# Two graph layers on one core: the squares moved into the aggregate's last pieces, the second layer's statistics put off by one more piece, one graph's channel sums and the second layer's weights read at other points

## The chip, the core and the metric

The kernel runs on one core of a Trainium2 chip. The core has a matrix engine (PE, with the weight loads shown apart as PEld), a vector engine (DVE), a scalar engine (ACT), a general engine (POOL) and a queue engine (SP) that only starts transfers; POOL starts transfers too. Every engine works through its own list of instructions in order and waits on semaphores for the others. The time is that of the whole program on the device, in microseconds; lower is better. Everything is float32.

## What is computed

Sixteen graphs of 1024 nodes with 256 channels share one 1024x1024 adjacency matrix. The first layer weighs the adjacency by a function of the channel means, forms queries from it, and does attention with four heads. The second layer multiplies by the normalised adjacency, applies a linear map, a normalisation over all graphs and nodes, a relu, a second linear map and a second normalisation.

```python
h = maximum(layernorm(x), 0)
c = mean(h, channels);  A = symmetric(2*||sigmoid(c_m - c_n) - .5| - .5|)
g = relu((h.T @ (adj * A)) * para)                 # queries, per graph
k, v = split(h @ kv_w);  x = x + softmax(g.T k) v  # 4 heads
h = maximum(layernorm(x), 0)
A_hat = dinv * (adj + I) * dinv                    # dinv from row and column sums
y1 = relu(batchnorm((A_hat @ h) @ W1.T + b1))
x = x + batchnorm(y1 @ W2.T + b2)
```

## The kernel before

One Python function records the instructions of all engines in the order in which they are to stand; nothing reorders them afterwards, so the order in the code is the order on each engine. The main body is `attention()`: for each graph b it goes through 16 steps of two score tiles and two value products, and between these it draws pieces from a generator, `background(b)`, which does everything else: keys, values and queries of graph b+1, and the second layer's aggregate (`aggregate`, seven products of a Strassen-like scheme, 14 pieces) and first linear map (`hidden`, two times seven products, 14 pieces) of graph b-1. In this text "stage b" is the stretch in which graph b has its attention. A stage in the middle takes some 135 us.

`weave(main, (start, side), ...)` takes one piece of each side generator with every piece of the main one, from piece number `start` on. `soon(action)` puts an action off until the next piece has been recorded: with one `soon`, an action stands on its engine behind the next piece's instructions. `weave`, `soon` and the counts in the calls are all that sets the order.

What the change touches:

- `squares(b)` (L432): two DVE transposes of 32x32 blocks (128x1024 each, L438), one for each half of the channels, into a tile `sq`, which a POOL transfer (L442) writes to DRAM; `gathered(b, k)` (L444) reads it back from there with four SP transfers (L450) as the transposed activations `ht` that the keys and values of the next stage take. `squares` is called in `prepare(b)` (L931) after two of `hidden`'s pieces, and it takes its tile from the pool tag "h" of two buffers, which also holds the activations of both layers.
- `summed(b)` (L926) is woven into the last eleven of the aggregate's pieces: the layernorm of graph b (eight pieces), then `differences(b)` (L454), which sends the channel sums through DRAM (L467) and reads them back as a row on all partitions, `cbc` (L471).
- `put` in `hidden` (L822) sends a finished 128x512 block of the second layer to DRAM and records its statistics (L825, DVE) one piece later. The products of `hidden` go to three PSUM buffers in turn (`bank`, L167): a product can start when the block of the product three before it has been taken out, which is done by DVE adds (L837, L842, L847, L860, L866) and ACT copies.
- `background(0)` (L949) weaves the queries of graph 1 with the pieces of `graph()` (POOL, the combined adjacency) and `degrees()` (column sums: loads of `at`, ACT at L241, DVE at L243 and L244), and calls `differences(2)` after all of them.
- `load_later()` (L303) reads the second layer's first weights (L305), forms four sums of them on POOL (L309 to L312), writes the 1024 values `dinv` to DRAM one by one (L314) and reads them back as a row on all partitions, `dbc` (L315), which has to wait for the write. It is called in stage 1, before the queries of graph 2. All its transfers stand on SP, in the same list as the loads of the adjacency (`adj`, L192), of `para` (L549) and of the aggregate's matrix (`aht`, L714).

Of the kernel before, what the change touches and what calls it, by code (L numbers as in the profile page):

```python
# [10 lines left out]
F32 = mybir.dt.float32  # L11
# [6 lines left out]
P = 128  # L18
# [5 lines left out]
def gnn_two_layers_kernel(  # L24
# [12 lines left out]
    nc = tc.nc  # L37
    B, N, C = x.shape
    H1 = w1_t.shape[1]
    NT = N // P  # L40
    CC = C // P
# [23 lines left out]
    stats1 = const.tile([P, HC, B * NH, 6], F32, name="stats1")  # L65
# [8 lines left out]
    hsq_d = [dram.tile([P, CC, N], F32, name=f"hsq_d{b}") for b in range(B)]  # L74
# [9 lines left out]
    SQ = 32  # L84
    NS = P // SQ
# [13 lines left out]
    def layers(shifted):  # L99
# [31 lines left out]
        def soon(action):  # L131

            queue.append(action)
# [17 lines left out]
        def weave(main, *sides):  # L151

            for i, cost in enumerate(main):
                for start, side in sides:
                    if i >= start:
                        cost += next(side, 0.0)
                yield cost
            for _, side in sides:
                yield from side

        def double(slots):

            for _ in slots:
                next(slots, None)
                yield 0.0
# [266 lines left out]
        def squares(b):  # L432

            sq = p2.tile([P, CC, N], F32, tag="h", name=f"sq_{b}")
            for k in range(CC):
                nc.vector.transpose(  # L438
                    sq[:, k].rearrange("p (i t s) -> p i t s", i=NS, s=SQ),
                    hs["a", b][:, :, k * P : (k + 1) * P].rearrange("p t (i s) -> p i t s", s=SQ),  # L440
                )
            nc.gpsimd.dma_start(out=hsq_d[b], in_=sq)  # L442

        def gathered(b, k):  # L444

            ht = p3.tile([P, N], F32, tag="ht", name=f"ht_{b}_{k}")
            hts.setdefault(b, []).append(ht)
            src = hsq_d[b][:, k].rearrange("(j s) (i r) -> i s j r", s=SQ, i=NS)
            for i in range(NS):
                nc.sync.dma_start(  # L450
                    out=ht[i * SQ : (i + 1) * SQ].rearrange("s (j r) -> s j r", j=NS), in_=src[i]
                )
# [342 lines left out]
        def hidden(b):  # L795

            if b >= B - 2:
                yield from plain_hidden(b)
                return
            HH = H1 // 2  # L800
            a11, a12, _, a22 = w1_quarters()
            s1, s2, s3, s4 = (later["s"][:, i] for i in range(4))
            b11, t3, b21, b22 = at_quarters(b)
            t1, t2 = steps[b]
            t4 = p2.tile([P, FB], F32, tag="para", name=f"at4_{b}")
            nc.gpsimd.tensor_sub(t4, b21, t2)

            def left(block, c):
                return block[:, c * P : (c + 1) * P]

            def one(name, block, c, right):
                part = bank(f"py_{b}_{c}_{name}")
                product(part, left(block, c), right, True, True)
                return part

            made = {}

            def new(name, c):
                made[name] = py.tile([P, FB], F32, tag="y", name=f"y_{b}_{c}_{name}")
                return made[name]  # L820

            def put(y, n, j):  # L822
                i = b * NH + n
                nc.gpsimd.dma_start(out=y1_d[i][:, j, :], in_=y)
                soon(lambda: nc.vector.bn_stats(stats1[:, j, i, :], y))  # L825

            add = nc.vector.tensor_add

            def m1(c):
                part = one("1", a11, c, b11)  # L830
                nc.scalar.activation(
                    new("11", c), part, AF.Identity, bias=b1[:, c : c + 1]
                )

            def m2(c):
                y = made["11"]
                add(y, one("2", a12, c, b21), y)  # L837
                put(y, 0, c)

            def m3(c):  # L840
                y = made["12"]
                add(y, one("3", s4, c, b22), y)  # L842
                put(y, 1, c)

            def m4(c):
                y = made["21"]
                add(y, one("4", a22, c, t4), made["sum"])  # L847
                put(y, 0, 2 + c)

            def m5(c):  # L850
                nc.scalar.copy(new("22", c), one("5", s1, c, t1))
                if c == 1:
                    both(c)

            def both(c):
                nc.gpsimd.tensor_add(new("12", c), made["21"], made["22"])

            def m6(c):
                y = new("21", c)
                add(y, one("6", s2, c, t2), made["11"])  # L860
                if c == 0:
                    both(c)

            def m7(c):
                part, y = one("7", s3, c, t3), made["22"]
                nc.vector.scalar_tensor_tensor(  # L866
                    new("sum", c), part, b1_step[:, c : c + 1], made["21"], op0=ALU.add, op1=ALU.add
                )
                nc.gpsimd.tensor_add(y, y, made["sum"])
                put(y, 1, 2 + c)  # L870

            for c, order in ((0, (m1, m5, m6, m2, m3, m7, m4)), (1, (m1, m6, m2, m5, m7, m3, m4))):
                for each in order:
                    each(c)
                    yield 0.86
# [50 lines left out]
        def summed(b):  # L926
            yield from Norm(b, True).all()
            differences(b)
            yield 0.0

        def prepare(b, products):  # L931


            w = weighers[b]
            yield from islice(products, 1)
            yield from islice(products, 1)
            squares(b)
            yield from weave(islice(products, 5), (0, islice(w, 2)))
            gathered(b, 0)
            yield from weave(islice(products, 3), (0, islice(w, 1)))  # L940
            gathered(b, 1)
            yield from weave(islice(products, 3), (0, islice(w, AHEAD - 3)))
            yield from products
# [3 lines left out]
        def background(b):  # L947

            if b == 0:  # L949
                differences(1)  # L950
                for k in range(CC):
                    yield TOP
                    transposed(1, (k,))
                    yield 1.0
                w, products, norm = weighers[1], keys_values(1), Norm(2, True).all()
                yield from weave(islice(products, 4), (0, double(islice(w, 8))))
                yield from weave(
                    plain_queries(1), (0, w), (4, norm), (5, graph()), (7, degrees())
                )
                differences(2)  # L960
                w = weighers[2]
                yield from islice(products, 1)
                yield from weave(islice(products, 2), (0, islice(w, 2)))
                yield TOP
                transposed(2, (0,))
                yield 1.0
                yield from weave(islice(products, 1), (0, islice(w, 1)))
                yield from islice(w, 1)
                yield TOP
                transposed(2, (1,))  # L970
                yield 1.0
                yield from islice(w, AHEAD - 4)
                yield from products
                return
            before = hidden(b - 1)
            gather = aggregate(b - 1)
            if b + 1 < B:
                w, products, norm = weighers[b + 1], keys_values(b + 1), normed(b - 1)
                yield from weave(islice(products, 4), (0, islice(w, 4)))
                if b == 1:  # L980
                    load_later()
                yield from weave(queries(b + 1), (0, double(w)), (9, islice(norm, 5)))
                yield next(gather)
                if b + 2 < B:
                    load_x(b + 2, True)
                yield from weave(products, (0, norm))
            else:
                yield next(gather)
                yield from weave(endings.pop(), (2, normed(b - 1)))
            if b + 2 < B:  # L990
                yield from weave(gather, (3, summed(b + 2)))
                yield from prepare(b + 2, before)
            elif b + 2 == B:

                yield from gather
                endings.append(before)
            else:
                yield from gather
                yield from weave(before, (0, normed_last()))
# [287 lines left out]
        with st:  # L1287
# [22 lines left out]
            else:  # L1310
# [7 lines left out]
                norm = Norm(0, True)  # L1318
# [369 lines left out]
```

## Time and profile before

| | |
|---|---|
| median of 3 runs | 2484.15 us (2481.71 to 2485.78) |
| the profiled execution | 2482.2 us, its span 2480.3 us |
| PE busy | 2418.3 us, 97% of the span |
| DVE busy | 1999.8 us, 81% |
| ACT busy | 1261.2 us, 51% |
| POOL busy | 565.2 us, 23% |

The page says that PE is busy in nearly the whole of the span. In the 40 slices PE stands at 9 tenths or more throughout, but for the last slice. So what an edit can give is found in the short stretches in which PE waits. The list of waits names them by the line that waited and the line that ended the wait; the timeline shows single instructions with start, duration, engine, line and, in brackets, the idle time before.

### The profile page before, as it was taken

To read this page: it belongs to the slowest core of one execution; us is meant where nothing else is said; L and a number is where in the kernel's file an instruction comes from. 1 tells how busy PE (TensorE), PEld (TensorE's weight loads), DVE (VectorE), ACT (ScalarE), POOL (GpSimd) and SP (SyncE) were. 2 spreads that over 40 slices of the span, in tenths; PEclk is the share of its full clock that TensorE was granted. 3 is DMA by queue.
4 is the path that set the end of the run, shared out by engine and by line. 5 is a ranking of instruction groups with operands and counts; after the bars stand their busy time and mean duration, and the time that the engine had idled before them with its cause. 6 is when DMAs were issued, how large, how long until landed. Compare 5 with 4: busy or idle time off the path is not lost. (4 is left out here: it accounts for less than half of the span.)

```text
span 2480.3 us, 35952 instructions
## 1 busy us (share of the span) xinstructions
PE 2418.3 (97%) x13290; PEld 829.3 (33%) x13290; DVE 1999.8 (81%) x3103; ACT 1261.2 (51%) x1870; POOL 565.2 (23%) x632
## 2 busy tenths in 40 slices
PE   9999999999999999999999999999999999999995
PEld 4333232332323232323323232323233232334444
DVE  5678887979798888889797978888897978767775
ACT  7764454545463645545454645355454534345554
POOL 1480202112121202021111212120201102136652
PEclk9999999999999999999999999999999999999997
DMA  4665535354555544453545555544535453456559
GB/s 145 198 218 175 181 124 191 120 198 157 181 174 191 168 168 162 144 181 118 210 143 175 170 191 170 187 160 148 177 126 197 133 199 122 157 205 222 192 198 373
DMA packets 202682, 437.19 MB, mean 176 GB/s; under 512 B 21248, under 2 KB 96512, under 8 KB 196736
## 3 DMA queue, kind: packets, MB, share of 16 engines
q1 hardware_dynamic: 173328, 327.29, 39.9%
q0 software_dynamic: 29168, 107.50, 11.4%
q8 instruction: 107, 1.75, 0.3%
q14 instruction: 79, 0.65, 0.1%
HBM read 331.36 MB, written 103.35 MB: 175 GB/s over the span
## 5 line engine op out<-in xcount | busy, mean ns | idle before, releaser
L1064 ACT ACTIVATE p<-sc 128x1024 f32<-128x1024 f32 x512 | 495.6, 1020 | 581.4 <-PE sc L1056 579.7
L1088 DVE TENSOR_TENSOR acc<-acc,p 128x1024 f32<-128x1024 f32 x384 | 469.5, 1223 | 81.6 <-ACT p L1064 60.3
L1056 PE MATMUL sc<-q,k 64*64 64x512 f32 x4096 | 500.1, 603 | 4.2 <-ACT p L1064 4.2
L1099 PE MATMUL o<-p,v 128*64 128x512 f32 x2048 | 494.6, 604 | 0.0
L174 PE MATMUL pa<-aht,h_b 128*64 128x512 f32 x1536 | 346.0, 592 | 1.1 <-ACT h_b L368 1.1
L174 PE MATMUL pg<-w,x_h 128*64 128x512 f32 x1472 | 332.0, 592 | 1.9 <-DVE x_h L579 1.9
L1056 PEld LDWEIGHTS sc<-q,k 64*64 64x64 f32 x4096 | 131.7, 132 | 340.9 <-issue 287.8
L1117 POOL DMA_DIRECT2D out_d<-os x58 | 33.9, 584 | 914.9 <-DVE os L1113 883.9
L1099 PEld LDWEIGHTS o<-p,v 128*64 128x64 f32 x2048 | 124.4, 136 | 297.9 <-issue 272.4
L493 DVE SCALAR_TENSOR_TENSOR w<-w,adj 128x1024 f32<-128x1024 f32 x128 | 166.2, 1306 | 31.9 <-ACT w L514 26.1
L174 PEld LDWEIGHTS pa<-aht,h_b 128*64 128x64 f32 x1536 | 110.0, 137 | 220.7 <-issue 208.8
L174 PEld LDWEIGHTS pg<-w,x_h 128*64 128x64 f32 x1472 | 105.6, 137 | 212.4 <-issue 201.0
L506 ACT ACTIVATE w<-cbc,csum 128x512 f32<-128x512 f32 x256 | 170.3, 716 | 4.7 <-DMA cbc<-csum_d 4.7
L514 ACT ACTIVATE w<-w 128x1024 f32<-128x1024 f32 x128 | 135.5, 1059 | 2.5
L569 DVE TENSOR_TENSOR w<-w,w 128x1024 f32<-128x1024 f32 x112 | 133.2, 1219 | 1.5
L174 PE MATMUL py<-at,w1s 128*64 128x512 f32 x448 | 109.5, 598 | 9.7 <-DVE y L837 7.5
L174 PE MATMUL pv<-kvw_f,ht 128*64 128x256 f32 x1024 | 116.1, 379 | 0.0
L174 PE MATMUL pk<-ht,kvw_f 128*64 128x512 f32 x512 | 115.2, 592 | 0.2 <-ACT ht L430 0.2
L174 PE MATMUL py<-at,w 128*64 128x512 f32 x464 | 113.3, 595 | 1.3 <-DVE at L727 0.7
L368 ACT ACTIVATE x_h<-x_h,lnsm_a 128x256 f32<-128x256 f32 x120 | 70.5, 593 | 74.6 <-DMA aht<-aht_d 67.1
L1085 DVE TENSOR_TENSOR acc<-p,p 128x1024 f32<-128x1024 f32 x64 | 79.2, 1237 | 31.5 <-ACT p L1064 31.5
L1428 ACT ACTIVATE yin_f<-yin_f,sm_f 128x512 f32<-128x512 f32 x128 | 93.5, 802 | 15.0 <-DMA yin_f<-y_d 14.9
(197 smaller groups left out, 2967.1 us busy)
## 6 DMA issues: line engine op xcount, KB each, us to landing
aht<-aht_d SPq DMA_DIRECT2D x224, 512.0 KB
adj<-in_adj_dram SPq DMA_DIRECT2D x128, 512.0 KB
y_d<-y POOLq DMA_DIRECT2D x128, 256.0 KB, 3.8
yin_f<-y_d SPq DMA_DIRECT2D x32, 1024.0 KB
para<-in_para_dram SPq DMA_DIRECT2D x64, 256.0 KB
x_d<-x_x POOLq DMA_DIRECT2D x16, 1024.0 KB, 5.1
xo_f<-x_d SPq DMA_DIRECT2D x32, 512.0 KB
out_dram<-xo_f POOLq DMA_DIRECT2D x32, 512.0 KB, 11.1
```

The lines of the kernel that those rows point to most:

```text
L174: nc.tensor.matmul(dst[r], left[:, r], right, start=start, stop=stop)
L368: nc.scalar.activation(self.h[:, t, :], self.src[:, t, :], AF.Relu, bias=self.sm[:, 1, t : t + 1], scale=self.sm[:, 0, t : t + 1], accum_o ...
L493: nc.vector.scalar_tensor_tensor(w, w, 1.0, a, op0=ALU.add, op1=ALU.mult)
L506: nc.scalar.activation(w[:, t, :].rearrange("p (t q) -> p t q", q=P), cbc[:, q * NT // NH : (q + 1) * NT // NH], AF.Abs, bias=csum[:, th * ...
L514: nc.scalar.activation(made[i], made[i], AF.Tanh, scale=-0.5 / C)
L569: nc.vector.tensor_sub(block(i)[part], block(x)[part], block(y)[part])
L1056: nc.tensor.matmul(sc[part, e, :], ks[b][k][r, m * P + c * HW : m * P + (c + 1) * HW], qs[b][k][r, f * FB : (f + 1) * FB], start=True, sto ...
L1064: nc.scalar.activation(pr, sc, AF.Exp)
L1085: nc.vector.tensor_add(self.acc, self.held, pr)
L1088: nc.vector.tensor_add(self.acc, self.acc, pr)
L1099: nc.tensor.matmul(self.o[r, :], vs[b][k][:, m, r], pr[:, e, :], start=(m == 0), stop=(m == NT - 1),)
L1428: nc.scalar.activation(y, y, AF.Relu, bias=sh[:, j : j + 1], scale=scale[:, j : j + 1])
```

## The change

Five edits:

1. `squares` becomes a generator of two pieces. Each half has a tile of its own tag "sq" with one buffer, its own transfer to DRAM, and a piece of its own.
2. It is called at the end of `summed`, beside the last two pieces of the aggregate, and no longer in `prepare`. There, `gathered(b, 0)` moves from after seven of `hidden`'s pieces to after two; `gathered(b, 1)` follows after eleven pieces where it followed after ten.
3. The statistics in `put` are put off by two pieces.
4. In `background(0)` the weave is cut after 13 of the 16 pieces of the queries, with 8 pieces of `graph` and 6 of `degrees`; then comes `differences(2)`, then the rest.
5. `load_later()` is called after the queries of graph 2, just ahead of the first loads of the aggregate.

```diff
-            sq = p2.tile([P, CC, N], F32, tag="h", name=f"sq_{b}")
             for k in range(CC):
+                sq = p1.tile([P, N], F32, tag="sq", name=f"sq_{b}_{k}")
                 nc.vector.transpose(
-                    sq[:, k].rearrange("p (i t s) -> p i t s", i=NS, s=SQ),
+                    sq.rearrange("p (i t s) -> p i t s", i=NS, s=SQ),
                     hs["a", b][:, :, k * P : (k + 1) * P].rearrange("p t (i s) -> p i t s", s=SQ),
                 )
-            nc.gpsimd.dma_start(out=hsq_d[b], in_=sq)
+                nc.gpsimd.dma_start(out=hsq_d[b][:, k], in_=sq)
+                yield 0.0
...
-                soon(lambda: nc.vector.bn_stats(stats1[:, j, i, :], y))
+                soon(lambda: soon(lambda: nc.vector.bn_stats(stats1[:, j, i, :], y)))
...
             yield from Norm(b, True).all()
             differences(b)
             yield 0.0
+            yield from squares(b)
...
             yield from islice(products, 1)
             yield from islice(products, 1)
-            squares(b)
-            yield from weave(islice(products, 5), (0, islice(w, 2)))
             gathered(b, 0)
+            yield from weave(islice(products, 6), (0, islice(w, 2)))
...
+                asked, build, sums = plain_queries(1), graph(), degrees()
                 yield from weave(
-                    plain_queries(1), (0, w), (4, norm), (5, graph()), (7, degrees())
+                    islice(asked, 13),
+                    (0, w),
+                    (4, norm),
+                    (5, islice(build, 8)),
+                    (7, islice(sums, 6)),
                 )
                 differences(2)
+                yield from weave(asked, (0, build), (0, sums))
...
+                yield from weave(queries(b + 1), (0, double(w)), (9, islice(norm, 5)))
                 if b == 1:
                     load_later()
-                yield from weave(queries(b + 1), (0, double(w)), (9, islice(norm, 5)))
                 yield next(gather)
```

## The prediction

> **What bounds the kernel.** The page comes first, then the list of waits for PE alone.
>
> ```profile
> PE 2418.3 (97%) x13290; PEld 829.3 (33%) x13290; DVE 1999.8 (81%) x3103; ACT 1261.2 (51%) x1870; POOL 565.2 (23%) x632
> ```
>
> ```profile
> PE py L174 <- DVE y L837: 7.5, 13, 0.6
> ...
> PE sc L1056 <- ACT p L1064: 4.2, 2, 3.7
> PE py L174 <- DVE y_sum L866: 2.2, 13, 0.2
> PE pg L174 <- DVE x_h L579: 1.9, 1, 1.9
> ```
>
> PE is the bound, and only its waits can be won. Two of the four rows come 13 times, once in each of stages 1 to 13, always equally long; the other two come once, in stages 0 and 1. These are the four places that the edits aim at. I then went through the timeline around each.
>
> Stage 1's `hidden`, on DVE, POOL and PE:
>
> ```profile
> 282.96 0.69 DVE L744 TENSOR_TENSOR at<-pa,at 128x512 f32<-128x512 f32 x1 [0.50 <-PE pa L174]
> ...
> 284.30 2.36 DVE L438 STREAM_TRANSPOSE sq<-x_h 128x1024 f32<-128x1024 f32 x2
> ...
> 287.54 1.29 POOL L856 TENSOR_TENSOR y<-y,y 128x512 f32<-128x512 f32 x1
> ...
> 289.28 2.55 DVE L1088 TENSOR_TENSOR acc<-acc,p 128x1024 f32<-128x1024 f32 x2
> ...
> 293.73 1.08 PE L174 MATMUL py<-at,w1s 128*64 128x512 f32 x4 [0.17 <-DVE y_sum L866]
> ...
> 301.82 1.08 PE L174 MATMUL py<-at,w1s 128*64 128x512 f32 x4 [0.57 <-DVE y L837]
> ```
>
> From L744 to L837 DVE has no gap above 0.3 us: PE waits for a full DVE queue. A product takes 0.86 us start to start (291.64 to 293.36 would be two), so the first stall is worth 0.37 and the second (due at 301.08, two products after 299.36) 0.74.
>
> Stages 0 and 1:
>
> ```profile
> 137.02 0.20 DVE L465 STREAM_TRANSPOSE csumt<-csum 128x32 f32<-128x32 f32 x1
> ...
> 148.26 1.33 ACT L506 ACTIVATE w<-cbc,csum 128x512 f32<-128x512 f32 x2 [4.70 <-DMA cbc<-csum_d]
> ...
> 152.05 3.40 PE L1056 MATMUL sc<-q,k 64*64 64x512 f32 x16 [3.71 <-ACT p L1064]
> ```
>
> ```profile
> 177.64 0.37 SPq L314 DMA_DIRECT2D dinv_d<-deg  x1
> ...
> 188.03 0.34 SPq L315 DMA_DIRECT2D dbc_f<-dinv_d  x1
> ...
> 196.46 1.23 DVE L493 SCALAR_TENSOR_TENSOR w<-w,adj 128x1024 f32<-128x1024 f32 x1 [4.75 <-DMA adj<-in_adj_dram]
> ```
>
> The row `cbc` comes late, ACT stands, and PE with it for 3.71 us; the scores after it take 3.40 where they take 1.95 elsewhere, because the granted clock is at half there. In stage 1 SP stands 10.4 us between L314 and L315 with two `adj` loads behind it; DVE waits 4.75 us for one, PE 1.95.
>
> **What the Trainium skill says.** "DMA: Bandwidth & Descriptors", "Rules for kernel authors": a transfer whose last dimension isn't contiguous has one descriptor per element, and one that reads what another wrote must wait for its semaphore. The trace agrees: 1024 values of 4 bytes took the 10.3 us above, and L315 waited. "SBUF — State Buffer", "SBUF: two separate sides": a DVE operation with two SBUF inputs and a GpSimd operation lock a shared port pair against each other, the later one blocks. Stage 2 shows it, where L856 happened to run over L1088:
>
> ```profile
> 424.31 1.29 POOL L856 TENSOR_TENSOR y<-y,y 128x512 f32<-128x512 f32 x1
> 424.75 3.27 DVE L1088 TENSOR_TENSOR acc<-acc,p 128x1024 f32<-128x1024 f32 x2
> ```
>
> The pair took 3.27 instead of 2.55, and PE lost 0.7 more in that stage. "TensorE: Matmul & The Clock Gate", "What's actually happening": an idle PE falls to half clock, about 3.4 us of work brings it back. The trace agrees once: 3.71 us idle cost 3.40 - 1.95 = 1.45 us more.
>
> **The change, part by part.** The orders of PE and ACT stay as they are; DVE, POOL and SP change.
>
> *Channel sums of graph 2.* L465 moves ahead of three pieces, behind L244 of the fifth `at` (ends 125.93). So `csum_d` starts at 126.1 instead of 137.25, and `cbc`, which followed it by 4.2 us and landed 6.8 us later, lands at about 137. ACT wants it at 143.6. The stall of 3.71 and its 1.45 us of half clock go: 5.2. On SP the last `at` load now stands behind these transfers; it starts near 130.7 instead of 125.9, and lands, 6 to 8 us later, at 137 to 139. ACT wants it at 132.42, so ACT stops there for some 5 us. Behind it stand L664, the two `v` copies and the next two exponentials, which end at 142 instead of 139.9; PE asks for their buffers at 144.5. The cover is 2.6 us; landing at 139 it costs up to 1.4 further on. I take 0.2. **Sum: -5.0.**
>
> *Second layer's weights.* The wait in stage 1's queries goes: -1.95. But L305, L314 and L315 now stand on SP just ahead of the five first `aht` loads. In stage 1 these start at 229.11 and PE takes the first at 239.87. In the later stages the whole SP sequence stands 2.1 us earlier against PE (last `para` 15.2 ahead of the first aggregate product, in stage 1 13.1, since DVE was behind there), and so it will here: the four `os` loads end at 227.0, L314 starts at 227.65, its write lands 10.3 us later, L315 starts at 238.0. A broadcast of this size landed 4.2 us after its start in the quiet stages (semaphore records of `cbc`), and `aht` blocks land 1.3 us apart (same records), so the first is there at 243.5. PE waits 3.6 us, and with the clock near the edge of falling I add 1.0 (none to 2). Both ends: the write 2 us quicker gives 1.6 in all, write and broadcast as slow as in stage 0 and 1 (10.3 after a later start, 6.8) 8. **Sum: -1.95 + 4.6 = +2.6.**
>
> *Squares and statistics* (13 stages). Nothing is removed: both transposes (1.22 each) and eight statistics (0.69) stay ahead of or behind the same L837. I replay stage 1's DVE with the timeline's durations. The first transpose goes between L787 and L1134 (278.57 to 279.79); what follows slips by 1.14 and fills the gap of 0.50 ahead of L744, which ends at 284.2. That is the buffer of the third product from 284.47: covered by 0.26. L727 ends at 284.93 for a product at 285.32: covered by 0.4. The second transpose can start at 284.86 if the first half's transfer, started at about 280.1, has left its single buffer: 4.8 us, where 256 KB of `out_d` took 2.4 and 1 MB of `hsq_d` 5.0 (medians of the page's transfers), so some 3.3 to 4.5 for 512 KB. It ends at 286.08, 0.58 sooner than now. L860 and L837 follow, L1134 and L1135, and L1088 is up at 288.7 instead of 289.28. On POOL the second transfer's issue now stands ahead of L806: issue at 286.4, L806 from 286.96 (before 284.46), L856 from 288.26 to 289.55 (before 287.54 to 288.83). So L856 is running when L1088 comes up, and DVE is blocked 0.7 us as in stage 2. The two L1088 end at 291.97; L842 ends at 292.57 (before 292.42), 0.1 late for PE; L866, which no longer has a statistic ahead of it, ends at 293.22 (before 293.67): that stall is gone. All four statistics of the first half, L860, L493 and two more L1088 still come ahead of the second half's L837, which ends at 301.55 instead of 301.76. PE goes on when it ends, so whatever was won before, the stage wins 0.21. Behind it, L842 now stands ahead of L493 and waits for L856 about 1 us, before products that need its buffer only 3 us later. 13 times 0.21 is 2.7, and stage 2 loses its extra 0.7: **-3.4.** `ht` needs nothing new: the first half is read earlier, the second waits for a product as now.
>
> Sum: -5.0 + 2.6 - 3.4 = -5.8 on the profiled execution's 2482.2 (span 2480.3): 2476.4. The median lies 1.95 above that execution: **2478**. A measurement of this kernel can tell some 0.2% (5 us) from no change.
>
> **Rivals.** *No collision on POOL* (L856 before or after L1088): then L837 ends 0.9 earlier instead of 0.21, 13 x 0.7 = 9 us more: 2469. For it: stage 1 to 13 but one have none now, and 0.5 us would do. Against: by the replay they overlap by 0.8.
>
> *The weights cost what was won*: the write lands as slowly as before after a later start, the broadcast takes 6.8, PE waits 6 us and then has half clock for 2. Then +6 instead of +2.6: 2482, no change that can be told. For it: the slow values are measured ones. Against: POOL's adjacency transfers shared the engines then.
>
> *The single buffer* (slower): if the first half's transfer takes over 4.8 us, DVE stands at the second transpose, and everything to L837 slips with it. Above 5.0 each stage loses; at 6.0 it is 1.0 x 13: 2491. The line to slower by over 0.2% is at 5.65. For it: 256 KB of `y_d` took up to 5.8 amid other loads. Against: only `cbc` is under way at that time, since SP waits for this very transfer.
>
> That the change doesn't do what it says is excluded by the order of instructions.
>
> **How the numbers follow.** My case 0.50, no collision 0.16, weights 0.24, single buffer 0.10. My case itself spans 2474 to 2483, with 0.8 of it under 2479.2; with no collision all of it, with the weights a tenth: faster 0.40 + 0.16 + 0.03, about 0.60. Slower only by the single buffer, 0.08. The rest, 0.32, is the same. Range: from no collision (2470) up to the weights at their worst (2485).
>
> **What would show it.** ACT L506 without its 4.7 us and scores at full clock at 150 us, in its place ACT L241 waiting for `at`; PE waiting about 3.6 us for `aht` at the first aggregate product, SP 10 us between L314 and L315 at that point; PE's wait for L866 gone 13 times, that for L837 still there, and L1088 pairs of 3.2 us beside L856. Wrong it would be by an idle DVE ahead of L438, by a wait for `aht` above 6 us or none, or by no wait at L837.

## The result, and the profile after

The changed kernel takes 2501.3 us (median, 2494.6 to 2503.4) against 2484.2 us before (2481.7 to 2485.8): the ratio is 1.0064, with a 95% interval of 1.0046 to 1.0081. It is slower by some 16 us by the ratio (17 between the medians), where 6 us less had been forecast. The profiled execution of the changed kernel has a span of 2500.1 us, 19.8 more than before.

The busy times hardly moved (first part of the page, changed kernel), so the time is in waits again:

```profile
PE 2422.9 (97%) x13290; PEld 832.7 (33%) x13290; DVE 2006.9 (80%) x3103; ACT 1260.6 (50%) x1870; POOL 559.9 (22%) x645
```

The list of waits for PE, changed kernel (who waited for whom: us in total, times, longest). Behind the squares the line numbers are larger by one than before, so that the old L837, L842, L860 and L866 are L838, L843, L861 and L867; in the attention itself they are larger by seven:

```profile
PE py L174 <- DVE y L838: 21.1, 13, 2.4
...
PE pa L174 <- DMA aht<-aht_d: 5.7, 1, 5.7
PE py L174 <- DVE y L843: 4.8, 12, 0.8
```

The wait of `sc` of 3.7 us and the rows for `pg` (1.9 once) and for `y_sum` L866 (13 times) are gone, as forecast. The row of the add of m2, once 7.5 us, has grown to 21.1, the first block of `aht` costs 5.7, and L843, waited for once before (0.5), comes 12 times.

To put the waits in one currency, I took from both traces how much later each group of matmuls starts after the one before than groups of that kind usually do, and added this up by stretch. The sums take in what half clock costs, and are good to some 2 us:

| PE's lost us | stage 0, scores | stage 1, queries | stage 1, first `aht` | stages 1 to 13 after that | all else |
|---|---|---|---|---|---|
| before | 5.3 | 2.1 | 0 | 14.8 | 18.7 |
| after | 0 | 0 | 8.2 | 34.2 | 17.9 |

The sum is 19.4 us more, nearly the 19.8 of the spans. So 7.4 us were won where they were looked for, 8.2 were lost at the first `aht` block, and 19.4 in the 13 stages. This last number is what had to be explained.

**Where the 13 stages lose it.** The timeline of stage 1 in the changed kernel (start, duration, engine, line; in brackets the idle time before):

```profile
285.81 1.25 DVE L438 STREAM_TRANSPOSE sq<-x_h 128x1024 f32<-128x1024 f32 x1
...
289.68 3.18 DVE L1095 TENSOR_TENSOR acc<-acc,p 128x1024 f32<-128x1024 f32 x2
290.37 0.57 POOL L825 DMA_DIRECT2D y_d<-y  x1
...
297.57 0.69 DVE L861 TENSOR_TENSOR y<-py,y 128x512 f32<-128x512 f32 x1 [1.08 <-PE sums L1155]
298.18 1.21 DVE L494 SCALAR_TENSOR_TENSOR w<-w,adj 128x1024 f32<-128x1024 f32 x1
...
302.93 0.68 DVE L838 TENSOR_TENSOR y<-py,y 128x512 f32<-128x512 f32 x1
```

The block of seven products is worked through twice in a stage; m1 to m7 are the products, and m6 in the second half is added by L861. DVE stands idle for 1.08 us ahead of it. In the kernel before the same add had no gap:

```profile
297.47 0.67 DVE L860 TENSOR_TENSOR y<-py,y 128x512 f32<-128x512 f32 x1
```

In the changed kernel the weights' multiplication (L494), a statistic and two accumulations come behind the late add, and only then L838, the add of m2, for which PE waits 1.95 us where it waited 0.74 (counted from when the product was due). The bracket names a matmul as releaser. The list of waits for DVE, changed kernel, gives another one for most of the stages:

```profile
DVE y L861 <- DMA y_d<-y: 8.6, 9, 2.2
DVE sq L438 <- DMA hsq_d<-sq: 5.7, 12, 0.9
```

The records of the transfers' semaphores agree with it: in each of the 13 stages L861 starts 0.12 us after the first `y_d` transfer of the stage has landed. L861 writes a new `y` tile; the tag has six buffers, and this is the seventh tile of the stage, so it takes the buffer that this transfer still reads. In the kernel before, the transfer landed 3.5 to 5.1 us after its start and 3.6 to 5.2 us ahead of the add; in the changed one it takes 6.1 to 8.2 us. The question is why.

SP's list, changed kernel and then before, in the same place of stage 1:

```profile
280.32 0.34 SPq L472 DMA_DIRECT2D cbc<-csum_d  x1
285.81 1.74 SPq L451 DMA_DIRECT2D ht<-hsq_d  x4
287.59 0.95 SPq L192 DMA_DIRECT2D adj<-in_adj_dram  x2
288.58 3.52 SPq L1130 DMA_DIRECT2D os<-out_d  x4
```

```profile
279.55 0.35 SPq L471 DMA_DIRECT2D cbc<-csum_d  x1
279.94 0.95 SPq L192 DMA_DIRECT2D adj<-in_adj_dram  x2
280.99 2.12 SPq L1123 DMA_DIRECT2D os<-out_d  x4
293.07 1.96 SPq L450 DMA_DIRECT2D ht<-hsq_d  x4
```

The read of `ht`, `gathered(b, 0)`, has moved ahead of two `adj` loads and four `os` loads, 1.25 MB. It waits for the first half of the squares to land (285.79), and SP with it. So these loads start 7.6 us later and run together with the transfer of the squares' second half and with `y_d`. The table by windows (us, busy time of PE, PEld, DVE, ACT, POOL, then the granted clock, the share of the DMA engines, GB/s), changed kernel from `y_d`'s start to its landing:

```profile
290.40:297.50 7.10, 7.03 (x46) 1.97 (x44) 5.99 (x8) 2.86 (x5) 3.47 (x6) 1.00 1.00 318
```

and the kernel before, likewise:

```profile
288.80:293.70 4.90, 4.76 (x24) 1.20 (x18) 4.80 (x7) 0.71 (x2) 1.08 (x3) 1.00 0.49 199
```

The DMA engines are full in one and half idle in the other. The Trainium skill says in general ("DMA: Bandwidth & Descriptors", "Issuing engines are not separate DMA queues") that transfers started by different engines share the same 16 DMA engines. POOL's `y_d` beside SP's loads agrees with it, 7.1 us in place of 4.9.

Two ends were open then: whether this late landing, and not the order of DVE, the single buffer of the squares or the statistics, is what costs the time; and how the five edits share it.

### The profile page after: what moved, and what is told of

Its sections match the earlier page's. It is cut to its first block, busy times and chain, and to the rows that moved or that the text cites. A ratio compares the mean times of both kernels' runs of the same rounds, so it can differ in the third digit from the quotient of the medians.

```text
span 2500.1 us, 35966 instructions
## 1 busy us (share of the span) xinstructions
PE 2422.9 (97%) x13290; PEld 832.7 (33%) x13290; DVE 2006.9 (80%) x3103; ACT 1260.6 (50%) x1870; POOL 559.9 (22%) x645
## 5 line engine op out<-in xcount | busy, mean ns | idle before, releaser
L1095 DVE TENSOR_TENSOR acc<-acc,p 128x1024 f32<-128x1024 f32 x384 | 479.8, 1250 | 76.7 <-ACT p L1071 55.1
L494 DVE SCALAR_TENSOR_TENSOR w<-w,adj 128x1024 f32<-128x1024 f32 x128 | 164.5, 1292 | 28.1 <-ACT w L515 27.0
L174 PE MATMUL py<-at,w1s 128*64 128x512 f32 x448 | 111.1, 604 | 21.5 <-DVE y L838 21.1
## 6 DMA issues: line engine op xcount, KB each, us to landing
out_dram<-xo_f POOLq DMA_DIRECT2D x32, 512.0 KB, 10.9
```

Source lines behind the costliest of these rows:

```text
L174: nc.tensor.matmul(dst[r], left[:, r], right, start=start, stop=stop)
L494: nc.vector.scalar_tensor_tensor(w, w, 1.0, a, op0=ALU.add, op1=ALU.mult)
L1095: nc.vector.tensor_add(self.acc, self.acc, pr)
```

## The experiments

The kernel before was measured again beside each group; its median was 2481.8, 2483.3, 2482.4 and 2483.7 us in the four groups. Ratios are to it, and can differ from the quotient of the medians by some 0.1%. In the lists, L837 to L840 are the same add of m2, whose line moves with the edits. "Lost" is PE's lost time as in the table above.

**1. The edits alone, on the kernel before.** The diffs are those of edit 4, edit 5, edit 3 and edits 1 and 2 above.

> The kernel before with the channel sums of graph 2 alone moved ahead. Theory: the wait of ACT for cbc in stage 0 goes, and with it PE's wait of 3.7 us and 1.5 us of half clock, 5.3 us in all: some 2478.9 us. Rival: ACT, waiting for the last load of the transposed adjacency instead, stops PE there as long: 2484.

2481.5 us, ratio 0.9995 (0.9988 to 1.0002): nothing won. The rival is right about the time and wrong about the place. The wait at 150 us is gone (lost 0 in place of 5.3), but stage 1's queries lose 8.8 in place of 2.1. Timelines of SP and DVE in this kernel:

```profile
176.80 0.37 SPq L314 DMA_DIRECT2D dinv_d<-deg  x1
185.45 0.34 SPq L315 DMA_DIRECT2D dbc_f<-dinv_d  x1
```

```profile
195.03 1.23 DVE L493 SCALAR_TENSOR_TENSOR w<-w,adj 128x1024 f32<-128x1024 f32 x1 [8.54 <-DMA adj<-in_adj_dram]
```

SP starts the write of `dinv` at 176.80, when POOL has finished it; in the kernel before it was 177.64. That time belongs to POOL's work on the combined adjacency and does not move when PE gets ahead. So PE arrives 5.3 us earlier at an `adj` load that comes hardly earlier. Edit 4 pays only together with something that takes `load_later` away from there.

> The kernel before with only the second layer's weights read later. Theory, from the trace of the changed kernel (PE 5.9 us for the first aht block and 2.3 us at half clock, against the 2.1 us won at the queries): 6.1 us slower, some 2490 us. Rival, the prediction's own sum: +2.6 us, 2487.

2484.3 us, ratio 1.0010 (1.0004 to 1.0017), 2.5 us slower, the prediction's own sum and not what I now expected. PE loses 5.9 us at the first `aht` block (4.0 of it waiting), less than in the changed kernel.

> The kernel before with only the statistics two pieces later. Theory: PE's wait for L866 goes (0.34 in each of 13 stages), its wait for L837 grows by the same, because all four statistics of the first half still come ahead of that add: 2484 us, no change. Rival: the statistics are what made the changed kernel slower, then some 10 us or more above before.

2477.6 us, ratio 0.9977 (0.9969 to 0.9986), 5.7 us faster by the ratio, with an interval from 3.5 to 7.7 (the medians lie 4.1 apart); neither theory nor rival. The list of waits for PE in this kernel has no row for L866, and the one for L837 did not grow:

```profile
PE py L174 <- DVE y L837: 7.8, 13, 0.6
```

A likely reason stands in the list of waits for DVE in the kernel before, in a row that is gone here: a statistic had itself been waiting for POOL's sum, on the engine that PE waits for.

```profile
DVE stats L825 <- POOL y L869: 11.2, 27, 0.6
```

The wait for L866 was worth 0.34 in each of 13 stages, 4.4 us in all, which the interval holds; by the sums of the trace the 13 stages lose 11.3 in place of 14.8.

> The kernel before with only the squares turned at the aggregate's end and prepare's new counts (edits 1 and 2). Theory: in all 13 stages of the changed kernel the add of the second half's m6 starts 0.12 us after the landing of the first y_d transfer, which takes 6.1 to 8.2 us where it took 3.5 to 5.1, because SP's loads start earlier and run beside it; the weights of the next graph then stand behind that add. With the statistics one piece later as before, DVE comes to that add some 0.7 us later, so the loss is somewhat under the 19 us of the whole: 10 to 15 us, 2494 to 2499 us, and that add starts at y_d's landing in most stages. Rival, from the prediction: the place of the transposes wins 0.2 us a stage, 2481.

2498.5 us, ratio 1.0058 (1.0045 to 1.0072), 14 us slower by the ratio, at the upper end of the range; the 13 stages lose 30.1, 15.3 more than before. So edits 1 and 2 alone bring most of the 19.4 lost there. In six stages L861 starts 0.12 us after `y_d`'s landing, in the others up to 1.4 after it, fewer than I expected. The rest of the loss is half clock in two stages and the adds of the first half, L843 late by 0.3 to 0.9 in each stage with the wait for L867 of 0.34 still behind it. And one clause of this expectation is wrong: SP's loads do not start earlier, as the list above shows, but later.

**2. What in edits 1 and 2 does it.** Four kernels, each the changed one with one thing different.

```diff
-        py = st.enter_context(tc.tile_pool(name=f"py_{kind}", bufs=6))
+        py = st.enter_context(tc.tile_pool(name=f"py_{kind}", bufs=7))
```

> The changed kernel with seven buffers of the tag y in place of six, nothing else. Theory: the add of the second half's m6 no longer takes the buffer that the first y_d transfer is still reading, so DVE does not stand ahead of it (mean 0.99 us a stage in the changed kernel, 12.8 us in 13 stages, and 3.0 us of half clock in stages 5 and 7): some 16 us faster than the changed kernel, 2485. Rival: what counts is only the order (the next graph's weights behind that add): 2501, no change.

2485.2 us, ratio 1.0007 (0.9999 to 1.0016), as the theory had it. `y_d` still takes 5.7 to 9.6 us, but in 12 of 13 stages L861 now starts ahead of its landing, without a gap:

```profile
PE py L174 <- DVE y L838: 7.8, 13, 0.6
...
PE py L174 <- DVE y L843: 4.9, 12, 0.9
```

The buffer that comes free late is shown as the cause of the greater part: the 13 stages lose 17.2 in place of 34.2. The wait for L843 is as large as in the changed kernel, and is another matter; it comes up again below. A page of the Trainium skill has the general form ("Perfetto Trace Analysis", "Optimization Strategy"): a gap that repeats can mean that there is no room for the next tile.

```diff
-            yield from weave(islice(products, 6), (0, islice(w, 2)))
+            yield from weave(islice(products, 5), (0, islice(w, 2)))
```

> The changed kernel with 5 in place of 6 pieces in prepare, so that the multiplication of the next graph's weights by the adjacency and a statistic stand ahead of the add of the second half's m6 again. Theory: this work (1.9 us) fills DVE's hole ahead of that add, and the add of m2 comes 3.6 us behind it in place of 5.3; with the landings of y_d as they are, stage by stage this gives 10.0 us and 2.6 us of half clock: some 12 us faster than the changed kernel, 2489. Rival: the order is indifferent, because DVE has the same work either way: 2501.

2487.8 us, ratio 1.0018 (1.0010 to 1.0026), 1 us from the number expected. With L494 and a statistic ahead of L861 there is work to do while `y_d` lands (a gap is left in four stages, 2.2 us in all, in place of 12.8), and L838 ends 4.9 us after L861's start where it ended 6.0 after it. So the count of pieces in `prepare` is a second condition: it takes the late landing and the order together to lose the whole of this time.

```diff
-            gathered(b, 0)
+            gathered(b, 1)
             yield from weave(islice(products, 6), (0, islice(w, 2)))
             yield from weave(islice(products, 3), (0, islice(w, 1)))
-            gathered(b, 1)
+            gathered(b, 0)
```

> The changed kernel with the two reads of the turned squares in exchanged order: SP asks for the second half first, waits for its transfer (landing some 7 us later) and only then starts the loads of the adjacency behind it; work and order of all other engines stay. Theory: y_d lands after 3.5 to 5.1 us as in the kernel before, where it took 6.1 to 8.2, because these loads no longer run beside it; DVE's hole ahead of m6's add closes: some 16 us faster than the changed kernel, 2485. Rival: y_d is slow by the second squares' transfer ahead of it on its own queue: it stays above 6 us, 2501.

2505.0 us, ratio 1.0084 (1.0070 to 1.0097). The first half of the theory holds: `y_d` lands after 3.1 to 4.5 us, and the gap ahead of L861 is gone. The second squares' transfer still stands ahead of `y_d` on POOL's queue, so it is SP's loads that made it late. The time does not follow, because the loads that make way are themselves waited for now. The list of waits for DVE in this kernel:

```profile
DVE w L494 <- DMA adj<-in_adj_dram: 28.3, 14, 2.9
```

Both places of SP's loads cost time once they are late: beside `y_d`, or behind it and late for L494.

```diff
-                sq = p1.tile([P, N], F32, tag="sq", name=f"sq_{b}_{k}")
+                sq = p2.tile([P, N], F32, tag="sq", name=f"sq_{b}_{k}")
...
-            turned = p1.tile([P, SQ], F32, tag="csumt", name=f"csumt_{b}")
+            turned = p1.tile([P, SQ], F32, tag="group", name=f"csumt_{b}")
...
-                    invs[b] = p2.tile([P, CC, NH, 2, 2, J], F32, tag="inv", name=f"inv_{b}")
+                    invs[b] = p1.tile([P, CC, NH, 2, 2, J], F32, tag="inv", name=f"inv_{b}")
```

> The changed kernel with two buffers for the squares (the room taken from two small tiles that get other buffers). Theory: the second transpose no longer waits for the first transfer (0.13 to 0.86 us, 5.7 in all); what stands behind it on DVE, and y_d's start on POOL, come as much earlier, so 5 to 6 us faster than the changed kernel, 2495. Rival, that the single buffer is the main cause: 13 us or more faster.

2504.3 us, ratio 1.0082 (1.0068 to 1.0096): nothing won. The second transpose's wait is gone, PE's wait for L843 has gone with it, and DVE waits longer for `y_d`:

```profile
DVE y L861 <- DMA y_d<-y: 23.5, 13, 2.6
```

Everything up to `y_d`'s start came earlier and its landing did not: `y_d` takes 6.3 to 8.6 us here. Counted from the landing of the first squares, which lets SP go on, `y_d` started 4.6 us later in the changed kernel and 4.1 on average here, and landed 11.6 and 11.9 us later on average.

**3. The weights, and whether the won time can be kept.** `load_later` split: weights and the write of `dinv` in the middle of the queries, the read behind them.

```diff
-                yield from weave(queries(b + 1), (0, double(w)), (9, islice(norm, 5)))
+                asked = weave(queries(b + 1), (0, double(w)), (9, islice(norm, 5)))
                 if b == 1:
+                    yield from islice(asked, 6)
                     load_later()
+                yield from asked
+                if b == 1:
+                    load_dbc()
```

> The changed kernel with the second layer's weights and the write of dinv in the middle of graph 2's queries (after six pieces) and only the read of dbc behind them. Theory: the changed kernel loses 8.2 us at the first aht block because SP stands 10.9 us for the write's landing with the aht loads behind it; with the write long landed nothing stands there, the cost of dbc ahead of aht being covered: some 8 us faster than the changed kernel, 2493. Rival: the wait there comes from the transfers' share of the DMA engines, not from SP's wait; then PE still waits 2 us or more for the first aht block.

2494.1 us, ratio 1.0042 (1.0028 to 1.0056); PE loses nothing at the first `aht` block. With the weights and the write started earlier SP no longer stands between it and the read (`dbc` starts at 220.5 in place of 230.7), so that stand was the cause there. The 13 stages lose 36.8, as in the changed kernel within the method.

> The kernel before with the channel sums ahead (edit 4) and the weights split like that. Theory: edit 4 alone won nothing because SP's stand at dinv, whose time POOL sets, kept the next adjacency loads where they were, so that stage 1 lost what stage 0 had won; with that stand gone from the queries, both waits go: 5.3 + 2.1 = 7.4 us faster than before. Rival: the two edits don't need each other, and this wins 2 us.

2474.3 us, ratio 0.9965 (0.9952 to 0.9979), 8 us faster. Stages 0 and 1 lose nothing up to the aggregate. Edit 4, worth nothing alone, is worth its 5 us here: it needs the other. Whether the split would win its 2 us alone was not run.

> The kernel of sums_split with the statistics two pieces later (edit 3): 13 times 0.34 more, as alone, so 12 us faster than before. Rival, from the prediction: no more than 0.2 a stage, 10 us.

2470.0 us, ratio 0.9948 (0.9934 to 0.9962): 4 us more than `sums_split`, as from 13 times 0.34. The intervals of the two ratios overlap, but the runs themselves do not: 2469.9 to 2470.4 us against 2474.1 to 2474.6, measured in one group. Laid beside those of `sums_split`, the score tiles move 4.4 us ahead over the 13 stages; the sums of lost time show only 2.5 of it.

```diff
-                soon(lambda: nc.vector.bn_stats(stats1[:, j, i, :], y))
+                soon(lambda: soon(lambda: soon(lambda: nc.vector.bn_stats(stats1[:, j, i, :], y))))
```

> The kernel of sums_split with the statistics three pieces later: one statistic (0.69) moves behind the second half's add of m2, for which PE waits 0.77 in each of 13 stages, so nearly all of that wait goes as well: some 9 us more than with two, 20 to 21 us faster than before, 2463. Rival: another wait takes its place (the y buffers are read later and come free later): no more than 12 us faster.

2465.9 us, ratio 0.9931 (0.9917 to 0.9945). The step is 4 us where 9 were expected, since PE's wait for m2's add halves and doesn't go (0.44 a stage in place of 0.77):

```profile
PE py L174 <- DVE y L839: 3.5, 13, 0.3
```

**4. The place of the read.** In the changed kernel the read of the squares goes back behind `adj` and `os`; then the same with two buffers for `sq` (the diff of `two_sq` above added); then all that paid, put together with the squares' move.

```diff
-            gathered(b, 0)
             yield from weave(islice(products, 6), (0, islice(w, 2)))
+            gathered(b, 0)
```

> The changed kernel with the first read of the turned squares back behind the six pieces, so that on SP two adjacency loads and four os loads (1.25 MB) stand ahead of it again, as in the kernel before. An earlier text had these loads start earlier in the changed kernel; its SP list says the opposite: they stand behind the read, which waits for the first squares' landing, and start at 287.6 where they started at 279.9, and so they run in y_d's time. Theory: with them back, y_d lands after some 3.5 to 5 us and DVE's hole ahead of m6's add goes, but the first squares' transfer now runs beside them, lands at 287 to 289, and the second transpose, with the single buffer, waits 2 to 4 us for it: the loss of the 13 stages moves to that place and stays, 2495 to 2515. Rival: the transfer stays near 5 us; then no wait is left and the kernel comes to 2485.

2525.6 us, ratio 1.0171 (1.0157 to 1.0185), the slowest of all. The mechanism is as expected and the size above the range. `y_d` lands after 3.2 to 5.9 us. But the first half's transfer, now beside the loads, takes 7.2 to 8.2 us (4.9 to 5.6 in the changed kernel), and DVE stands at the second transpose. The lists of waits for DVE and for PE in this kernel:

```profile
DVE sq L438 <- DMA hsq_d<-sq: 39.8, 13, 3.4
```

```profile
PE py L174 <- DVE y L843: 38.3, 13, 3.2
```

> The same with two buffers for the squares. Theory: the second transpose waits for nothing, y_d lands early, both holes are gone: the stretch of the 13 stages loses some 1 us a stage as in the kernel before, and the kernel comes to 2485 or a little less (16 us faster than the changed one). Rival: the squares' transfers, now beside the loads, make ht or y_d late in another place: above 2492.

2478.2 us, ratio 0.9980 (0.9974 to 0.9987): 23 us below the changed kernel, 7 more than expected. Neither wait is left (`y_d` 4.3 to 5.6 us, and L861 no earlier than 0.45 us after its landing); each stage loses 0.77:

```profile
PE py L174 <- DVE y L838: 7.8, 13, 0.6
```

There is no row for L843 here, as in `two_sq`. These two kernels have two buffers for the squares, and POOL's L857 runs over an accumulation of DVE in every stage in them as in the changed kernel (one of 1.83 us in place of 1.22). So the wait for L843, 7 us in the 13 stages of the changed kernel and of `seven_y`, belongs to the single buffer, not to that collision.

The windows also limit what can be said of `y_d`. Here the DMA engines are as full during it as in the changed kernel, and it takes 4.7 us in stage 1 where it took 7.1:

```profile
290.12:294.85 4.73, 4.73 (x24) 1.34 (x20) 4.63 (x6) 0.49 (x2) 1.91 (x4) 1.00 1.04 315
```

So full engines alone do not make it late. In this kernel SP's loads start 7 us earlier than in the changed one; how much of them was still under way when `y_d` started was not followed.

> The fastest kernel so far (channel sums ahead, split weights, statistics three pieces later, 2465.9) with the squares at the aggregate's end as well, with two buffers, the reads back and five pieces in prepare. Theory: with both holes gone the squares' place is worth little: PE's wait for m2's add (0.44 a stage) shrinks by up to 0.2: 2462 to 2466. Rival: POOL's addition still runs beside DVE's accumulation as in the changed kernel and costs 0.3 to 0.6 a stage: 2470.

2466.3 us, ratio 0.9932 (0.9919 to 0.9946), the same as `plus_statistics_3` without the squares' move; PE's wait for m2's add is 0.44 a stage here and there. So beside these edits the squares' new place is worth nothing that can be measured, even when all that it brought along is mended.

PE's lost time in all the kernels, by stretch as above:

| kernel | stage 0 | queries | first `aht` | 13 stages | time, us |
|---|---|---|---|---|---|
| `alone_sums` | 0 | 8.8 | 0 | 14.8 | 2481.5 |
| `alone_weights` | 1.8 | 0 | 5.9 | 14.8 | 2484.3 |
| `alone_statistics` | 4.1 | 1.8 | 0 | 11.3 | 2477.6 |
| `alone_squares` | 1.6 | 7.7 | 0 | 30.1 | 2498.5 |
| `seven_y` | 0 | 0 | 7.6 | 17.2 | 2485.2 |
| `five_pieces` | 0 | 0 | 7.3 | 20.4 | 2487.8 |
| `reads_held` | 0 | 0 | 8.2 | 38.3 | 2505.0 |
| `two_sq` | 0 | 0 | 8.0 | 43.0 | 2504.3 |
| `after_split` | 0 | 0 | 0 | 36.8 | 2494.1 |
| `sums_split` | 0 | 0 | 0 | 15.0 | 2474.3 |
| `plus_statistics_2` | 0 | 0 | 0 | 12.5 | 2470.0 |
| `plus_statistics_3` | 0 | 0 | 0 | 8.4 | 2465.9 |
| `reads_back` | 0 | 0 | 7.6 | 59.2 | 2525.6 |
| `reads_back_two_sq` | 0 | 0 | 8.1 | 10.2 | 2478.2 |
| `best_with_squares` | 0 | 0 | 0 | 7.8 | 2466.3 |

## Why the prediction was wrong

**Channel sums: right, but not on its own.** ACT waited 4.45 us for the last `at` load, which ended at 136.9, and began the row of `w` at 143.41, against 5 us, 137 to 139 and 143.6 in the prediction. PE lost nothing by it and won 5.3 us (5.0 forecast). What was missed: the sum added this to the 1.95 us of the next edit as if each stood alone. Alone it is worth nothing, since what POOL's time sets in stage 1 takes back what stage 0 gives. It cancels in the sum only because the changed kernel has both edits.

**Weights: the wait that came was the one forecast, its size was off.** +2.6 was forecast; in the changed kernel's trace it is 8.2 - 2.1 = +6.1. Three terms were small by a little each. The write took 10.9 us in place of 10.3. The first `aht` block landed 7.5 us after the start of the `dbc` read in place of 5.5: the estimate added a quiet broadcast and one block, and the block took 7.1 us, `dbc` itself 6.3. Half clock cost 2.3 in place of 1.0. This is the rival "the weights cost what was won", to a tenth, in the whole kernel; in the kernel before the edit alone costs 2.5, near the forecast. Part of that nearness is luck: in that kernel's trace PE loses 5.9 at the first `aht` block against the 4.6 forecast.

**Squares and statistics: wrong, and this decided it.** -3.4 was forecast, and the 13 stages lost 19.4 more. By the experiments this is 17.0 for the buffer of `y` (34.2 against 17.2 in `seven_y`), 7.0 for the single buffer of the squares (17.2 against 10.2 in `reads_back_two_sq`, which has neither wait, with the read moved back) and 4.6 won by the later statistics (10.2 against 14.8 before). The step that failed is the replay of stage 1, at "L860 and L837 follow", with its closing sentence that "`ht` needs nothing new: the first half is read earlier". The replay checked DVE's order, POOL's order and the PSUM buffers. It did not ask of L860 where its output tile comes from, and it did not ask of the moved read what stands behind it on SP. Both are in the profile of before: L860 started 3.8 us after `y_d`'s landing in stage 1 (3.6 to 5.2 in the others), and SP's list shows the `adj` and `os` loads that the read was moved past. With both, the chain follows: the read waits for the squares, 1.25 MB of loads starts 7.6 us later, `y_d` needs 6 to 8 us among them, and the margin of 3.6 to 5.2 us is used up, the more so as DVE comes to that add earlier with L493 no longer ahead of it. That all the work "still comes ahead of the second half's L837" was true and not enough: a queue with the same work ends later if a wait in its middle leaves a gap.

A second step was mis-sized: 3.3 to 4.5 us for the first half's transfer, within the 4.8 of cover. It took 4.9 to 5.6, so DVE stood 0.13 to 0.86 us ahead of the second transpose, and PE was 0.23 to 0.96 late at L843 in every stage, 0.54 on average, where 0.1 had been forecast and put down to POOL.

Smaller steps of this part. The collision of POOL's L857 with the accumulation came as forecast (3.18 us for the pair in stage 1), and by the two kernels with two buffers PE pays nothing for it. The wait for L866 went in all 13 stages. The sentence that the stage wins only 0.21, whatever was won before, fell too: alone, the later statistic won the 0.34 of that wait, and the wait for L837 did not grow.

**The rivals.** "No collision on POOL" is out. "The single buffer" was right in form and is the smaller of the two losses: the transfer takes 4.9 to 5.6 us against the break-even of 5.0, and this costs 0.54 a stage. Taking this wait away alone wins nothing, since `y_d`'s landing holds DVE behind it. (Its two prices count from different starts: 2491 at 6.0 us counts from 5.0, the line at 5.65 from 4.8. And the slowest `y_d` in the trace of before took 6.4 us, not 5.8.) The argument against it was right as well, that SP starts nothing beside that transfer because it waits for it; but SP's waiting was itself the loss. With the read where it had been, the rival comes true in full, DVE waiting 3.1 us a stage: the changed order protects the single buffer at the cost of everything behind it on SP. No rival held SP's loads against a buffer of `y`, so the main loss lay outside all of them, and the range of 2470 to 2485 missed 2501 by 16 us.

**Still open.** `alone_weights` loses 2.3 us less at the first `aht` block than the changed kernel does. By SP's lists its write holds SP for 0.7 us less (10.35 against 11.01), and PE's first product follows the start of the `dbc` read 1.0 us sooner (6.64 against 7.68); why these two transfers were quicker there is open. What lengthens `y_d` beside SP's loads, if the engines' share does not tell it, is open too.

## What to carry to other kernels

A transfer that waits on an in-order queue delays all that stands behind it: when a read is moved ahead, list what it is moved past, where those transfers then run, and which buffers are freed by transfers that share the time with them. In a replay, check every instruction for four things, its inputs, its engine, its PSUM buffer and the tile that it writes; margins as regular as 3.6 to 5.2 us in 13 stages look like nothing until something spends them. And an edit that gains in one place is worth only what the next fixed time downstream lets through: here an edit worth nothing alone and one that cost 2.5 us alone gave 8 us together, once the second was split.

## What the runs showed of the hardware

The time of a transfer depended on its company as much as on its size. 512 KB of squares took 4.9 to 5.6 us with little beside them (changed kernel) and 7.2 to 8.2 beside 1.25 MB of loads (`reads_back`). The first `y_d` transfer of a stage, 256 KB, took 3.1 us at best and 9.6 at worst. An earlier start among SP's loads bought nothing: in `two_sq` it was started 0.5 us sooner, on average, and landed no sooner. The busy share of the DMA engines did not tell its time: at a share of 1.00 to 1.04 it took 7.1 us in the changed kernel's stage 1 and 4.7 in that of `reads_back_two_sq`.

After waits of PE of 2.44 us in stages 5 and 7 of the changed kernel the matmuls behind ran at half clock and cost 1.4 to 1.6 us more; after one of 2.21 us in stage 12 they did not. In `alone_squares` a wait of 1.97 us (stage 13) was enough, so no length of waiting from which the clock falls can be read from these.

POOL's addition L857 running over a DVE accumulation made that one take 1.83 us in place of 1.22, in each of the 13 stages of the changed kernel.
